# Two graph layers in fp32: the products of Q and K issued with 128 moving columns instead of 256

## The chip, the cores and the metric

The kernel runs on one core of a Trainium2 chip. The metric is the device time of one execution in microseconds (us). The engines are called as the profile calls them: PE is the matrix engine (its MATMUL instructions), PEld is its other row, on which the weight loads (LDWEIGHTS) stand, DVE is the vector engine, ACT the scalar engine, POOL is GpSimd, and SP is the engine whose queue issues most of the transfers.

## What is computed

There are 64 graphs of 256 nodes with 512 features, and an adjacency matrix of 256 x 256 for each. Two attention layers follow one another; all data are fp32.

```
# layer 0: one score per pair of nodes, masked by adj
feat_proj = feats @ fc_w.T + fc_b
logits = q(feat_proj) + k(feat_proj)^T ;  masked = leaky(logits + (1 - adj) * -1e9)
x1 = softmax(masked) @ feat_proj + feats
# layer 1: eight heads of 64
Q = x1 @ W_q + b_q ; K = x1 @ W_k + b_k ; V = x1 @ W_v + b_v
scores = Q_h @ K_h^T / 8 + (a_i + c_j + b_g) + log(adj + 1e-9)
out = softmax(scores) @ V_h (heads side by side) + x1
```

## The kernel before

**Tiling.** Two graphs make a group of 512 tokens, so there are 32 groups. Every pass of the main loop (`step`, L1107) works on up to four groups at once: it finishes group d, does layer 1 of group a, layer 0 of group f and loads group n. The order of all instructions on all engines is written out by hand: `attention_and_layer_0` (L1068) and `step` issue pieces such as `pq.p7` or `factor:2:0` one after the other, and each engine carries out its own instructions in that order.

**The big products.** Four products of 512 tokens x 512 features x 512 features are made for a group: pf (layer 0 features), pq (Q), pk (K) and pv (V). Each is done as a 2 x 2 block product with seven instead of eight block products (Strassen's scheme in Winograd's form). A block is 256 x 256. DVE makes the sums of blocks beforehand (`xsum`, L374, and `ysum`, L349) and adds the results afterwards (`sum`, L442). `Product.add` (L401) issues one block product: two halves m of 128 output rows, two steps k of 128 along the contraction, so 4 calls of `matmul` (L412), each with a stationary block of 128 x 128 and 256 moving columns. With `rows` true (pf and pv) the tokens are stationary and the weights move; with `rows` false (pq and pk) a block of weights is stationary and the 256 columns that move are tokens: 128 of each of the two tiles t of a graph (TPG is 2). The result of a block product fills one PSUM bank: two halves m of 256 columns each. Where the moving block is a block of x1 itself, its columns lie in pieces of 32 (`moving`, L380), else in rows of 128 (`by_chunks`, L361).

Each call of `matmul` on fp32 data becomes two pairs on the chip, each pair a LDWEIGHTS and a MATMUL: the profile counts 512 MATMULs for a kind of pq product of which the program issues 8 calls in each of 32 groups.

**What stands around pq and pk in the order.** In `step`, after pf has ended, comes `pq.p1 pq.keep_1 pk.p1 pk.keep_1 pv.p1 pv.keep_1`, then the remaining block products of pq and pk in the order p6, p7, p2, p5, p3, p4 of pq, mixed with those of pk (L1131 to L1148), then pv. After each, ACT copies the bank (`read`, L426) or DVE adds it to a copy (`sum`, L442). PSUM has a pool of four banks (`bank`, L179) and a pool of two pairs of banks (`pair`, L182). Layer 1 goes on with the scores (`sc`, L859), the exponential on ACT (L873), the multiplication with the adjacency on DVE (L879) and the product with V (`oT`, L899). Layer 0 makes `y` (L689) and then pf. A small product `rc` (L637), with 80 moving columns, makes sums of weights. In the first group there are transposes by PE (`xTp` L705, `pfc` L152, `qrow` L581, `x1Tp` L811), each with 128 moving columns[...].

Of the kernel before, what the change touches and what calls it, by code (L numbers as in the profile page):

```python
# [17 lines left out]
P = 128  # L18
# [7 lines left out]
def kernel(  # L26
# [64 lines left out]
    nc = tc.nc  # L91
# [3 lines left out]
    B = 32  # L95
    RS = P // 4
    NC = D // P
    TPG = N // P
# [65 lines left out]
    def fast():  # L164
        main = ExitStack()
        with main:
# [222 lines left out]
            class Product:  # L389
# [11 lines left out]
                def add(self, n, dst, start):  # L401

                    a, b = a_w[self.a][n], self.b[n]
                    l, r = (b, a) if self.rows else (a, b)
                    for m in range(2):
                        for k in range(2):
                            o, lk, rk = dst[:, m], l[:, k], r[:, k]
                            if len(rk.shape) == 3:
                                o = o.rearrange("p (t n) -> p t n", t=TPG)
                            elif len(rk.shape) == 4:  # L410
                                o = o.rearrange("p (t a m) -> p t a m", t=TPG, m=B)
                            nc.tensor.matmul(  # L412
                                o, lhsT=lk[:, ts(m, P)] if len(lk.shape) == 2 else lk[:, m], rhs=rk,
                                start=(start and m == 0 and k == 0), stop=(m == 1 and k == 1),
                                skip_group_check=True,
                            )

                def fresh(self, n, scores=False):
                    name = f"{self.name}_{n}"
# [750 lines left out]
            with tc.manual_schedule(engines=ENGINES):  # L1170
# [9 lines left out]
                d, a, a_w = None, None, {}  # L1180
                for g in range(NG):
                    n = Group(g + 1) if g + 1 < NG else None
# [7 lines left out]
                    d, a, f = a, f, n  # L1190
# [215 lines left out]
```

## Time and profile before

| what | value |
|---|---|
| time, median of 2 runs | 2311.41 us (2310.98 and 2311.84) |
| span of the profiled execution, first to last instruction | 2308.8 us |
| time of the profiled execution itself | one of the two runs; the page gives only its span, 2.2 to 3.0 us under their times |
| PE busy (MATMUL) | 2294.2 us, 99% of the span, 12618 instructions |
| PEld busy (LDWEIGHTS) | 1905.2 us, 83%, 12618 instructions |
| DVE busy | 2124.2 us, 92% |
| ACT busy | 1071.8 us, 46% |
| POOL busy | 121.9 us, 5% |
| mean share of the 16 DMA engines, queue q1 | 28.8% |
| mean granted clock of PE | 0.997 of full speed |

How to read the profile: a line of a group gives the line of the program, the engine, the operation, what it writes and reads, the number of instructions, and behind the bars the busy time in us with the mean of one in ns, and the idle time of the engine just before them. For PE the duration of a MATMUL goes from its start to a modelled end, and consecutive MATMULs overlap; so the time that a MATMUL costs in a stream is the distance from one start to the next, which the timeline and the chain of work give, and not the duration of one. In the timeline a row "start, us, engine, line, operation, xcount" covers count instructions from the first start to the last end; with the duration of one known, the distance of two starts is (us minus the duration of one) divided by (count minus 1).

### The profile page before, as it was taken

To read this page: it belongs to the slowest core of one execution; us is meant where nothing else is said; L and a number is where in the kernel's file an instruction comes from. 1 tells how busy PE (TensorE), PEld (TensorE's weight loads), DVE (VectorE), ACT (ScalarE), POOL (GpSimd) and SP (SyncE) were. 2 spreads that over 40 slices of the span, in tenths; PEclk is the share of its full clock that TensorE was granted. 3 is DMA by queue.
4 is the path that set the end of the run, shared out by engine and by line. 5 is a ranking of instruction groups with operands and counts; after the bars stand their busy time and mean duration, and the time that the engine had idled before them with its cause. 6 is when DMAs were issued, how large, how long until landed. Compare 5 with 4: busy or idle time off the path is not lost.

```text
span 2308.8 us, 33613 instructions
## 1 busy us (share of the span) xinstructions
PE 2294.2 (99%) x12618; PEld 1905.2 (83%) x12618; DVE 2124.2 (92%) x3180; ACT 1071.8 (46%) x1865; POOL 121.9 (5%) x120
## 2 busy tenths in 40 slices
PE   9999999999999999999999999999999999999997
PEld 6888888888888888888888888888888888888885
DVE  6899999999999999999999999999999999999997
ACT  3544444454445444454444454444544445444443
POOL 0000000000000000000000000000000000000000
PEclk9999999999999999999999999999999999999999
DMA  4122332223322233232233232332222323223312
GB/s 133 46 61 73 78 76 66 70 61 85 79 73 61 61 78 78 74 68 61 69 78 83 60 75 63 79 78 74 64 60 74 78 73 70 65 64 81 84 46 38
DMA packets 517264, 163.84 MB, mean 71 GB/s; under 512 B 415188, under 2 KB 478696, under 8 KB 517096
## 3 DMA queue, kind: packets, MB, share of 16 engines
q1 hardware_dynamic: 514440, 160.32, 28.8%
q8 instruction: 102, 1.67, 0.3%
q10 hardware_dynamic: 2656, 1.31, 0.2%
q14 instruction: 66, 0.54, 0.1%
HBM read 95.43 MB, written 66.12 MB: 70 GB/s over the span
## 4 chain that ended last, share of the span: by engine, by line
PE 98%; DVE 1%; DMA 0%; ACT 0%; issue 0%; ACTq 0%; DVEq 0%
PE pv L412 17%; PE pq L412 17%; PE pf L412 16%; PE pk L412 16%; PE sc L859 11%; PE oT L899 10%; PE y L689 9%; PE fp L718 1%; DMA fc_nat<-in_L_gnn_fc_w_dram 0%; PE rc L637 0%; DVE osb L1034 0%; PE tot L927 0%; DVE osb L1040 0%; PE xTp L705 0%; DVE osb L1033 0%; DVE x L756 0%
## 5 line engine op out<-in xcount | busy, mean ns | idle before, releaser
L873 ACT ACTIVATE e<-sc,c 128x1024 f32<-128x1024 f32 x254 | 269.0, 1110 | 79.2 <-PE sc L859 77.6
L879 DVE TENSOR_TENSOR e<-e,am 128x1024 f32<-128x1024 f32 x254 | 297.7, 1213 | 0.4 <-ACT e L873 0.4
L859 PE MATMUL sc<-qT,kT 64*128 64x256 f32 x2048 | 255.8, 390 | 0.3 <-ACT e L873 0.3
L899 PE MATMUL oT<-e,v 128*64 128x256 f32 x2032 | 233.4, 382 | 0.0
L859 PEld LDWEIGHTS sc<-qT,kT 64*128 64x128 f32 x2048 | 187.3, 187 | 52.6 <-issue 32.7
L495 POOL TENSOR_TENSOR pf_s<-pf_s,x 128x512 f32<-128x512 f32 x93 | 118.4, 1273 | 2106.1 <-ACT pf_s L494 2038.8
L689 PE MATMUL y<-e,x 128*128 128x256 f32 x992 | 225.6, 381 | 0.0
L899 PEld LDWEIGHTS oT<-e,v 128*64 128x64 f32 x2032 | 140.2, 137 | 85.3 <-issue 10.7
L689 PEld LDWEIGHTS y<-e,x 128*128 128x128 f32 x992 | 186.4, 190 | 23.7
L432 ACT ACTIVATE pq_s<-pq,cols 128x256 f32<-128x256 f32 x192 | 80.5, 470 | 249.1 <-PE pq L412 249.1
L494 ACT ACTIVATE pf_s<-pf,recip 128x256 f32<-128x256 f32 x186 | 77.9, 470 | 197.6 <-PE pf L412 197.6
L917 DVE TENSOR_REDUCE part<-est 128x32 f32<-128x1024 f32 x124 | 151.3, 1220 | 4.3
L916 DVE STREAM_TRANSPOSE est<-es 128x1024 f32<-128x1024 f32 x124 | 152.2, 1227 | 0.0
L886 DVE TENSOR_TENSOR es<-e,e 128x1024 f32<-128x1024 f32 x126 | 149.3, 1205 | 1.1
L695 ACT COPY yT<-y 128x512 f32<-128x512 f32 x124 | 72.6, 585 | 131.7 <-PE y L689 130.9
L429 ACT COPY pk_s<-pk 128x512 f32<-128x512 f32 x96 | 56.3, 586 | 165.7 <-PE pk L412 159.0
L906 ACT COPY oTs<-oT 128x512 f32<-128x512 f32 x128 | 75.0, 586 | 118.0 <-PE oT L899 97.3
L412 PE MATMUL pk<-t1b,wk 128*128 128x256 f32 x512 | 121.1, 380 | 0.4 <-DVE kT L443 0.4
L412 PE MATMUL pv<-wv,t1b_c 128*128 128x256 f32 x512 | 121.1, 380 | 0.0
L412 PE MATMUL pv<-wv,t1b 128*128 128x256 f32 x512 | 121.0, 380 | 0.0
L412 PE MATMUL pq<-x1T,wq 128*128 128x256 f32 x512 | 121.0, 379 | 0.0
L412 PE MATMUL pk<-x1T,wk 128*128 128x256 f32 x512 | 121.0, 379 | 0.0
(181 smaller groups left out, 4506.3 us busy)
## 6 DMA issues: line engine op xcount, KB each, us to landing
x<-in_x_dram SPq DMA_DIRECT2D x32, 1024.0 KB, 5.1
out_dram<-osb SPq DMA_DIRECT2D x254, 128.0 KB, 3.1
xd<-xt SPq DMA_DIRECT2D x124, 256.0 KB, 2.0
x1T<-xd SPq DMA_DIRECT2D x496, 64.0 KB, 1.9
adj<-in_adj_dram SPq DMA_DIRECT2D x128, 128.0 KB, 3.5
qrow<-q SPq DMA_DIRECT2D x31, 256.0 KB, 3.9
fc_nat<-in_L_gnn_fc_w_dram ACTq DMA_DIRECT2D x4, 256.0 KB, 3.8
wq<-in_L_gnn_W_q_dram SPq DMA_DIRECT2D x1, 1024.0 KB
```

The source lines that it names most:

```text
L412: nc.tensor.matmul(o, lhsT=lk[:, ts(m, P)] if len(lk.shape) == 2 else lk[:, m], rhs=rk, start=(start and m == 0 and k == 0), stop=(m == 1 ...
L432: nc.scalar.activation(dst[:, m], src[:, m], AF.Identity, bias=self.bias[:, 2 * o + m : 2 * o + m + 1],)
L494: nc.scalar.mul(s[:, m], src[:, m], self.recip[:, TPG * k + m : TPG * k + m + 1])
L495: nc.gpsimd.tensor_tensor(s, s, self.out(o, k), ALU.add)
L689: nc.tensor.matmul(y[:, ts(gr, N)], lhsT=self.x[:, gr * TPG + j, ts(c, P)], rhs=self.e0[:, j, gr, :], start=(gr == 0 and j == 0), stop=(gr ...
L859: nc.tensor.matmul(sc[:, par, pr, :], lhsT=self.kT[rows, 2 * hg + pr, ts(t, P)], rhs=self.qT[rows, 2 * hg + pr, ts(gr, N)], start=True, st ...
L873: nc.scalar.activation(e, sc, AF.Exp, bias=self.c[:, t : t + 1], scale=SCALE)
L879: nc.vector.tensor_tensor(ef, ef, self.am[:, jc, u // 2, :].unsqueeze(1).to_broadcast([P, 4, N]), ALU.mult,)
L886: nc.vector.tensor_tensor(self.esum[u], self.e[u, 0], self.e[u, 1], ALU.add)
L899: nc.tensor.matmul(oT[par * HD : (par + 1) * HD, pr, :], lhsT=self.v[:, gr * TPG + jc, ts(h, HD)], rhs=self.e[2 * gr + hg, jc][:, par, pr, :],
L916: nc.vector.transpose(turned, self.esum[u].rearrange("p a b i -> p (a b i)"))
L917: nc.vector.tensor_reduce(self.part[:, hg, :], turned.rearrange("p (m c) -> p m c", c=B), AX.X, ALU.add,)
```

## The change

In `Product.add`, for the products that are not `rows` (pq and pk), each call with 256 moving columns becomes two calls with 128 moving columns, one for each tile t of the graph. Both have the same stationary block, and each loads it for itself. They write the two halves of the columns that the one call wrote. The flag `start` stands on the first of them only where it stood before, and `stop` on the last. pf and pv are issued as before. No other engine's instructions and no order of pieces is changed.

```diff
                         for k in range(2):
                             o, lk, rk = dst[:, m], l[:, k], r[:, k]
-                            if len(rk.shape) == 3:
-                                o = o.rearrange("p (t n) -> p t n", t=TPG)
-                            elif len(rk.shape) == 4:
-                                o = o.rearrange("p (t a m) -> p t a m", t=TPG, m=B)
-                            nc.tensor.matmul(
-                                o, lhsT=lk[:, ts(m, P)] if len(lk.shape) == 2 else lk[:, m], rhs=rk,
-                                start=(start and m == 0 and k == 0), stop=(m == 1 and k == 1),
-                                skip_group_check=True,
-                            )
+                            lk = lk[:, ts(m, P)] if len(lk.shape) == 2 else lk[:, m]
+                            first, last = start and m == 0 and k == 0, m == 1 and k == 1
+                            if self.rows:
+                                nc.tensor.matmul(
+                                    o, lhsT=lk, rhs=rk, start=first, stop=last,
+                                    skip_group_check=True,
+                                )
+                                continue
+                            for t in range(TPG):
+                                ot = o[:, ts(t, P)]
+                                rt = rk[:, ts(t, P)] if len(rk.shape) == 2 else rk[:, t]
+                                if len(rt.shape) == 3:
+                                    ot = ot.rearrange("p (a m) -> p a m", m=B)
+                                nc.tensor.matmul(
+                                    ot, lhsT=lk, rhs=rt, start=first and t == 0,
+                                    stop=last and t == TPG - 1, skip_group_check=True,
+                                )
```

## The prediction

> **What bounds the kernel now.** I read the page's parts 1 and 4 first, then the chain of work in order of time for one middle group, then the rows of the weight loads, then the few places where PE already runs short matmuls.
>
> ```profile
> span 2308.8 us, 33613 instructions
> PE 2294.2 (99%) x12618; PEld 1905.2 (83%) x12618; DVE 2124.2 (92%) x3180; ACT 1071.8 (46%) x1865; POOL 121.9 (5%) x120
> PE 98%; DVE 1%; DMA 0%; ACT 0%; issue 0%; ACTq 0%; DVEq 0%
> ```
>
> The chain that ended last is PE for 98%. Busy time of PE says little by itself (ends are modelled), but the list of waits confirms it: PE's longest wait is 5.0 us, at the very end, and all its other waits together are under 5 us. DVE is busy for 92%, yet nobody waits for it long. So a microsecond more or less in PE's stream is a microsecond of the whole.
>
> ```profile
> 1037.97 6.91 PE pq L412 x32
> 1044.88 1.73 PE pk L412 x8
> 1046.60 3.45 PE pq L412 x16
> 1050.06 8.63 PE pk L412 x40
> ```
>
> These are pieces of the chain: start, length, count. Each is count x 216 ns (6.91 / 32 = 0.216), without gaps: the MATMULs of pq and pk follow each other every 216 ns. [...]
>
> ```profile
> L412 PEld LDWEIGHTS pq<-t1b,q_s 128*128 128x128 f32 x512 | 97.5, 190 | 13.0
> L412 PEld LDWEIGHTS pk<-x1T,k_s 128*128 128x128 f32 x256 | 48.7, 190 | 6.5
> ```
>
> Each MATMUL has its own load of 128 x 128, of 190 ns, which starts when the MATMUL before it starts and lies wholly beside it. pq has rows of 512 (x1T,wq), 512 (t1b,wq), 512 (t1b,q_s) and 256 (x1T,q_s): 1792. pk has the same. Together 3584 pairs, 3584 x 0.216 = 774.1 us, a third of the span.
>
> [...]
>
> **What the change does, part by part.** The listing of the changed program has, for pq and pk, eight 128 x 128 calls where there were four of 128 x 256, in the same places with the same waits; ACT, DVE, POOL and SP have their instructions in the old order, and no transfer is added but the fetching of a longer PE program. So:
>
> 1. Streaming: 3584 MATMULs of 216 become 7168 [...]. The transposes show it:
>
> ```profile
> 37.44 0.60 PE L811 MATMUL x1Tp<-ident,x 128*128 128x128 f32 x4
> ```
>
> Four starts in 0.60 us with 273 ns for the last: (0.60 - 0.273) / 3 = 109 ns. Streaming alone: 7168 x 109.2 = 782.7 us, 8.6 more than 774.1. The columns are the same[...].
>
> 2. Loads: 3584 more, and the cover for each halves from 216 to 109 ns. A transpose's load takes only 140 ns, so it is not proof for the 190 ns kind. Two places are nearer. Behind those transposes come ordinary loads:
>
> ```profile
> 37.44 0.36 PEld L811 LDWEIGHTS x1Tp<-ident,x 128*128 128x128 f32 x3 [0.29 <-issue]
> 37.77 0.30 PEld L750 LDWEIGHTS x1p<-v,e 128*128 128x128 f32 x2
> ```
>
> The two x1p loads take 0.30 us together, and each lasts about 190 ns, so they start 110 ns apart: the second starts as its predecessor's weights go into use, under a transpose of 128 columns. The other is the small product rc, with 80 columns (69 ns of streaming), where the load and not the stream must be the limit:
>
> ```profile
> 1008.90 0.41 PEld L637 LDWEIGHTS rc<-part,every 128*128 128x128 f32 x2
> 1009.23 0.30 PEld L689 LDWEIGHTS y<-e,x 128*128 128x128 f32 x2
> ```
>
> ```profile
> 1009.12 0.34 PE L637 MATMUL rc<-part,every 128*128 128x80 f32 x2
> 1009.30 0.42 PE L689 MATMUL y<-e,x 128*128 128x256 f32 x1
> ```
>
> The first rc load starts at 1008.90, the second 0.41 - 0.19 = 0.22 later (at 1009.12), y's first at 1009.23, its second 0.30 - 0.19 = 0.11 later. So with only 80 columns to hide in, full loads follow each other every 110 to 112 ns (all 31 groups show 109 to 113, read from the starts in ns); the y MATMUL lasts 0.42 instead of 0.38 us because it waits for its load, 0.04. [...] So a load occupies its path for about 111 ns[...]. [...]
>
> ```profile
> 1.86 2.25 PEld L1176 LDWEIGHTS warm<-ident 128*128 128x128 f32 x10
> ```
>
> Ten loads of 334 ns each, fp32 128 x 128, before MATMULs of 128 columns: (2.25 - 0.334) / 9 = 213 ns apart. The page's clock row shows full speed here, but a load of 334 ns instead of 190 doesn't[...].
>
> I take 111 ns per new pair. Sum: 7168 x 111 = 795.6, minus 774.1 = +21.5 us. Ends of this row: 110 gives +14.4, 112 gives +28.7. Only rc's short runs show the fp32 load as limit at full clock, hence the bounds for a long stream: 109.2 below (+8.6), and above, [...] the whole 190 (+588). [...]
>
> 3. Everything else, costed at nothing: ACT and DVE read the banks as before. Each bank is ready 16 x 111 - 8 x 216 ns = 0.05 us later, and the next piece of PE comes that much later too. In the stretch 1030.8 to 1058.6 DVE is busy for 24.1 of 27.8 us; it gets about 0.6 us more room in every group. If a bank's reader were late by more than its cover, PE would wait for it, but a slower PE lengthens the cover. The end after the last PE product (some 10 us of DVE and stores) stays.
>
> 4. Fetching the program: queue q8 brings 1.67 MB in 102 packets, about PE's 25236 instructions; 7168 more are 0.46 MB on queues that are 0.3% busy. PE will take an instruction every 55 ns through pq and pk; oT does so already (32 pairs in 3.60 us, 56 ns an instruction) without a wait.
>
> Against the profiled execution: 2308.8 + 21.5 = 2330.3 us of span. The median of the runs is 2.6 above the span: 2311.4 + 21.5 = 2332.9 us, 0.9% more. A measurement of this kernel tells about 2% from no change, so this falls within 2%.
>
> **The rivals.**
>
> A (the forecast), 0.70: load-limited at 110 to 112, 2325.8 to 2340.1 us.
>
> B, 0.12: the steady stream is limited by the columns alone, 109.2: 2320 us. [...] Against: rc's 111. If the builder or PE dropped the second load of the same block (the change then not doing what it says) the time would be this one too[...].
>
> C, slower by over 2%, 0.12: in a long stream the loads are not overlapped. Place: each LDWEIGHTS of pq and pk. Price: [...] the full 190 ns gives 2899 us. It decides from 114.5 ns per pair on (+46 us). For it: the load's duration of 190[...]. Against: rc's 31 groups and x1p's 110.
>
> D, slower as well, 0.04: the longer program arrives late. 7168 instructions in packets of 16 KB are 28 more packets; at 3.8 us each (the median landing of fc_nat, as an estimate) and with PE standing still each time, +106 us on top of A, 2439 us. Against: oT's rate without a wait, and queues that are nearly idle.
>
> What remains, 0.02, is for what I don't see; half of it I give to faster.
>
> **How the numbers follow.** The likeliest is A at 111: 2332.9. Its own range is 2325 to 2341. The range for 8 in 10 takes in B below and C's milder edge above up to its deciding point: 2317 to 2357, which holds A and B, 0.82. Faster by over 2%: 0.01. Within 2%: A, B and the rest, 0.83. Slower: C and D, 0.16.
>
> **What will show it.** PEld's count goes to 16202 and so does PE's. A chain piece of pq with 16 MATMULs should last 1.78 us (A), 1.75 (B)[...], where 8 last 1.73 now. MATMULs of pq and pk should last about 275 ns (273 plus a wait of a few). pf, pv, y, sc and oT keep their 216 spacing, and no wait of PE for ACT or DVE grows. I am wrong if loads at full clock with no slack at all need more than the 112 that short runs show, or if waits between the banks' readers and PE appear.

## The result and the profile after

| | before | after |
|---|---|---|
| median time, first measurement | 2311.41 us (2 runs) | 2339.84 us (2338.61 and 2341.06) |
| ratio | | 1.0122, 95% interval 1.0103 to 1.0141 |
| median time, second measurement | 2311.53 us (9 runs) | 2338.36 us (4 runs) |
| ratio | | 1.0114, 95% interval 1.0099 to 1.0130 |
| span of the profiled execution | 2308.8 us | 2339.3 us |

The kernel is slower by 1.1 to 1.2%. The head of the page after:

```profile
span 2339.3 us, 40781 instructions
...
PE 2323.5 (99%) x16202; PEld 2023.4 (86%) x16202; DVE 2126.0 (91%) x3180; ACT 1071.9 (46%) x1865; POOL 121.9 (5%) x120
...
q8 instruction: 129, 2.11, 0.4%
...
PE 98%; DVE 1%; DMA 1%; ACT 0%; issue 0%; SPq 0%; DVEq 0%
```

Both rows of PE have 3584 instructions more, the other engines none. The longer program is 27 packets more on q8 (the queue that brings the instructions), and the chain is still PE for 98%. The same pieces of the chain of one group, in order of time (start, length, engine, what, line, count):

```profile
1052.84 7.14 PE pq L421 x64
1059.98 1.79 PE pk L421 x16
1061.77 3.57 PE pq L421 x32
1065.34 8.93 PE pk L421 x80
1074.28 6.91 PE pv L411 x32
```

Now pq's 64 MATMULs take 7.14 us, 111.6 ns each, where 32 took 6.91; pv, which was not cut, keeps 216 ns (6.91 / 32). From the starts in the trace, in ns, 99% of the distances between MATMULs of pq and pk are 111 or 112; two of three are 112, so the mean is 111.67 ns. Before it was 215.83. The weight loads, by form:

```profile
L421 PEld LDWEIGHTS pq<-t1b,q_s 128*128 128x128 f32 x1024 | 119.4, 192 | 1.7
L421 PEld LDWEIGHTS pk<-t1b,k_s 128*128 128x128 f32 x1024 | 119.5, 192 | 0.0
```

The idle time before these loads, 13.0 us a row before, is all but gone (1.7 and 0.0), and as each load lasts 192 ns and they start 111.67 apart, consecutive ones overlap. For the MATMULs of pq the page after has 275 ns each, 3 more than the 272 to 273 of a transpose with as many columns. That fits a wait of 2.5 ns of each for its load (111.67 against 109.2, the mean distance of the transposes of both kernels at full clock).

The sum of the difference: from the first MATMUL of pq to the last of oT the profiled executions take 2253.4 us before and 2280.6 after, +27.2; 7168 x 111.67 - 3584 x 215.83 = 800.4 - 773.5 = +26.9. The first pq starts 3.1 us later in this execution (46.37 after 43.31). That belongs to this execution's start and not to the change: another profiled execution of the changed kernel, in the second measurement, started it at 43.83 and took 2280.6 us for the same stretch. About 1.4 us of the 3.1 are there when the first transposes of x start (10.99 after 9.55), with 1.2 us of waits for arriving data (0.3 before). Most of the rest comes up to 19.90 (16.85 before): between 16 and 20 us the granted clock was 0.52, and 1.00 before. The tail differs by 0.2 us.

### The profile page after: what moved, and what is told of

Read it like the earlier page. It is cut to its first block, busy times and chain, and to the rows that moved or that the text cites. A ratio compares the mean times of both kernels' runs of the same rounds, so it can differ in the third digit from the quotient of the medians.

```text
span 2339.3 us, 40781 instructions
## 1 busy us (share of the span) xinstructions
PE 2323.5 (99%) x16202; PEld 2023.4 (86%) x16202; DVE 2126.0 (91%) x3180; ACT 1071.9 (46%) x1865; POOL 121.9 (5%) x120
## 4 chain that ended last, share of the span: by engine, by line
PE 98%; DVE 1%; DMA 1%; ACT 0%; issue 0%; SPq 0%; DVEq 0%
PE pq L421 17%; PE pv L411 17%; PE pk L421 17%; PE pf L411 16%; PE sc L867 10%; PE oT L907 10%; PE y L697 9%; PE fp L726 1%; DMA x<-in_x_dram 0%; PE rc L645 0%; DMA xd<-xt 0%; PE pfc L152 0%; PE xTp L713 0%; DVE osb L1042 0%; PE tot L935 0%; DVE osb L1048 0%
## 5 line engine op out<-in xcount | busy, mean ns | idle before, releaser
L451 DVE TENSOR_TENSOR qT<-pq,pq_s 128x512 f32<-128x512 f32 x96 | 66.1, 689 | 64.9 <-PE pq L421 33.7
L421 PE MATMUL pq<-x1T,wq 128*128 128x128 f32 x1024 | 124.9, 275 | 0.2 <-DMA x1T<-xd 0.2
L421 PE MATMUL pk<-t1b,wk 128*128 128x128 f32 x1024 | 124.9, 275 | 0.2 <-DVE kT L451 0.2
L421 PE MATMUL pk<-x1T,wk 128*128 128x128 f32 x1024 | 124.8, 275 | 0.0
L421 PE MATMUL pq<-t1b,wq 128*128 128x128 f32 x1024 | 124.8, 275 | 0.0
```

The source lines that it names most:

```text
L421: nc.tensor.matmul(ot, lhsT=lk, rhs=rt, start=first and t == 0, stop=last and t == TPG - 1, skip_group_check=True,)
```

## The experiments

Theory 1: a pair of LDWEIGHTS and MATMUL costs the larger of two times, streaming (0.833 x N + 2.5 ns for N moving columns) and the load of the next block (0.833 x c + 5 ns for c stationary columns). The first is a line through the 215.83 ns of 256 columns and the 109.2 of the transposes with 128; two more distances of the kernel before lie on it, 69 ns between the two MATMULs of rc (80 columns, by the line 69.2) and 429 between those of fp (512 columns, 429.2). The second is an estimate: 111.67 at 128 columns is the change's, and its slope was taken to be that of the first, for no other width of a load had been measured as a limit. For 128 and 128 the two times are 109.2 and 111.7 ns, so the load decides. Theory 2: the load is hidden, and every MATMUL of the cut products has a fixed 5 ns above its columns (111.67 less 128 x 0.833). Theory 3: the supply of PE's instructions sets the pace.

The code below shows the lines that matter, without their indentation; `...` stands for lines left out.

**Uneven pieces.** As many pairs and columns as in the change, but 192 + 64, from both tiles t (where x1 itself moves, three and one of its four pieces of 32):

```diff
-for t in range(TPG):
-    ot = o[:, ts(t, P)]
-    rt = rk[:, ts(t, P)] if len(rk.shape) == 2 else rk[:, t]
...
+o = o.rearrange("p (t n) -> p t n", t=TPG)
+pieces = [(o[:, :, s], rk[:, :, s]) for s in (slice(0, 96), slice(96, 128))]
...
```

> Q's and K's calls of 256 columns are cut into 192 + 64 instead of 128 + 128; same number of pairs, loads and columns as in the change. Theory 1 [...]: [...] the 64 pairs are held at 111.7 ns by the load behind them; 3584 x (162.5 + 111.7) - 3584 x 215.8 = +209 us, about 2520 us. Theory 2 (each MATMUL costs its columns plus a fixed 5 ns, whatever the load): same as the change, +27 us, about 2339 us.

Measured: 2519.6 us, before 2311.5; ratio 1.0901, interval 1.0881 to 1.0921; +208.1 where theory 1 had +209 and theory 2 +27. The chain of this kernel:

```profile
1053.30 8.72 PE pq L427 x64
1062.02 2.19 PE pk L427 x16
```

136.3 ns for each MATMUL in the mean, the mean of 162.5 and 111.7 being 137.1 (the edges of a piece of the chain take off a little). By form, in the same kernel:

```profile
L427 PE MATMUL pq<-t1b,q_s 128*128 128x192 f32 x512 | 137.6, 350 | 0.0
L427 PE MATMUL pq<-t1b,q_s 128*128 128x64 f32 x512 | 84.7, 247 | 0.0
```

The starts in ns show how the halves of a call interleave. Each call makes two pairs with the same columns, so the order is 192, 192, 64, 64. The distance after a 192 is 162 or 163 when a 64 comes next, and 218 or 219 when a 192 does (63 times in 1792, at the head of a run, 162 or 163); it is 55 or 56 from a 64 to a 64, and 111 or 112 from a 64 to a 192. By theory 1 they should be 162.5, 162.5, 111.7 and 111.7; the start noted for a MATMUL behind a 64 comes early, as with rc (its second MATMUL starts 69 ns after the first, though the load of 190 ns in front of it began only with the first), so only the sum counts: 162.5 + 218.3 + 55.8 + 111.7 = 548.3, which is what theory 1 has. So the same number of pairs, loads and columns costs 180 us more once a part of the pairs has only 64 columns to cover a load. Theory 2 falls. (The 55.8 ns from a 64 to a 64 are the 0.833 x 64 + 2.5 of streaming.)

**Quarters.** Four pieces of 64 columns (32 from each tile t), against the uneven kernel:

```diff
-pieces = [(o[:, :, s], rk[:, :, s]) for s in (slice(0, 96), slice(96, 128))]
+pieces = [(o[:, :, s], rk[:, :, s]) for s in [ts(n, B) for n in range(4)]]
...
```

> The calls are cut into four of 64 columns, 14336 pairs instead of 3584, each with a full load. Theory 1 (load-limited, 111.7 ns per pair whatever the columns): 14336 x 111.67 - 773.5 = +827 us, about 3139 us. Theory 2 (columns plus fixed 5 ns): 14336 x 58.3 - 773.5 = +63 us, about 2374 us. Theory 3 (it is the supply of instructions to PE that sets the pace): at most as slow as theory 1, and the same time with shorter loads.

Measured: 3137.9 us; ratio 1.3577, interval 1.3552 to 1.3601; +826.4, theory 1 had +827. Half the columns per pair, the same time per pair (14.24 / 128 = 111.3 ns):

```profile
1012.32 3.57 PE pk L427 x32
...
1017.68 14.24 PE pq L427 x128
1031.91 3.57 PE pk L427 x32
```

**Shorter loads.** The change with 96 stationary columns in most calls:

```diff
+c = P if start and k == 0 else 96
...
-ot, lhsT=lk, rhs=rt, start=first and t == 0,
+ot[0:c], lhsT=lk[:, 0:c], rhs=rt, start=first and t == 0,
```

> As the change (128 + 128 columns), but each load and MATMUL of Q and K has only 96 stationary columns, except the 6 of 28 calls that begin a bank; a quarter of most sums of Q and K is left out. Theory 1: [...] these pairs go at 109.2 ns: 5632 x 109.17 + 1536 x 111.67 - 773.5 = +12.8 us, about 2324 us. Theory 2 (fixed cost per MATMUL) and theory 3 (instructions): as the change, +27 us, about 2339 us.

Measured: 2325.1 us, ratio 1.0060, interval 1.0047 to 1.0074; +13.6, theory 1 had +12.8 and the others +27. In the chain, pq's 32 at one go are now 3.49 / 32 = 109.1 ns each, the 109.2 of streaming; pk's first 16, half of which have full loads, lie between at 1.77 / 16 = 110.6:

```profile
1111.89 1.77 PE pk L426 x16
...
1115.39 7.03 PE pq L426 x64
1122.41 1.75 PE pk L426 x16
1124.16 3.49 PE pq L426 x32
```

From the starts in ns, a 96-wide pair is followed after 109 or 110 ns and a 128-wide one after 111 or 112. So two prices make up the change's 26.9 us: 3584 more MATMULs at 2.5 ns each, 9.0 us (7168 x 109.17 - 773.5), which stay when the loads are short, and 7168 x 2.5 ns = 17.9 us because full loads follow each other every 111.67 ns where 128 columns stream in 109.17. Of the 13.6 left here, 12.8 are the 9.0 and the 1536 pairs that kept their full loads (3.8); the interval is wider than the rest. In this kernel the MATMULs are narrower too, not only the loads. That the load is the cause fits the transposes of the kernel before: 128 wide, with 128 columns and shorter loads of 140 ns, they follow each other every 109 ns.

**Quarters with shorter loads.** Four pieces of 64 columns with 64 stationary columns, `c = P if start and k == 0 else 64`.

> Four calls of 64 columns as in the quarters kernel, with loads and MATMULs of only 64 stationary columns except the 6 of 28 calls that begin a bank; half of most sums of Q and K is left out. Theory 1: [...] 11264 x 58.3 + 3072 x 111.7 - 773.5 = +226 us, about 2538 us. Theory 2: as the quarters kernel by theory 2, about 2374 us. Theory 3 (supply of instructions): as the quarters kernel measures, since the instructions are as many.

Measured: 2657.1 us, ratio 1.1496, interval 1.1475 to 1.1517; +345.6, which none of the theories had. Theory 3 falls (345.6 against the quarters' 826.4 with as many instructions). Theory 1 is right in the steady stretches, where MATMULs 64 wide follow each other every 58 or 59 ns (theory 1 has 58.3 for the load and 55.8 for streaming), but short by 119 us in all. The surplus sits where the stationary width changes between 128 and 64: 205 ns from the last 128-wide to the first 64-wide MATMUL, 152 the other way, and once more 107 or 160 behind. There are 832 such changes, 143 ns each. The 96-wide loads showed nothing of the sort. This made a theory 4: a change between 128 and 64 stationary columns can't be covered.

**Widths that change with every call, and seldom.** Both kernels are the kernel before, with 256 moving columns, but for the width of Q's and K's calls:

```diff
+c = P if self.rows or k == 0 else P // 2               # alternating
+c = P if self.rows or (start and k == 0) else P // 2   # mostly 64
...
-o, lhsT=lk[:, ts(m, P)] if len(lk.shape) == 2 else lk[:, m], rhs=rk,
...
+o[0:c], lhsT=lk[:, 0:c], rhs=rk, start=first, stop=last,
```

> The kernel before with its 256 moving columns, but in Q's and K's products every call with k = 1 has only 64 of the 128 stationary columns (half of those sums is left out), so the width changes with every call: 4 changes in each of 448 block products, 1792 in all; 1792 of 3584 pairs have the shorter load. Theory 4 (a change of the stationary width between 128 and 64 can't be covered: the load behind it waits for the running MATMUL; 143 ns per change from the surplus of the quarters-with-64 kernel, 119 us over 832 changes, and 100 to 200 ns as the scores' pieces of the kernel before show): +180 to +360 us. Rival (the 64-wide loads themselves were slow in that kernel): here they hide under 216 ns of streaming, so 0 us.

> As the alternating kernel, with 256 moving columns, but 64 stationary columns in all of Q's and K's calls except the 6 of 28 that begin a bank: 2816 of 3584 pairs have the shorter load (half of these sums is left out), with only 832 changes of width. Theory 4: 832 / 1792 of what the alternating kernel loses, +83 to +166 us. Rival (short loads are slow): 2816 / 1792 = 1.6 times what it loses.

Measured: 2616.6 us, ratio 1.1322 (1.1289 to 1.1355), and 2451.6 us, ratio 1.0608 (1.0577 to 1.0639). That is +305.4 and +140.5 over the 2311.1 of before. The ratio of the two is 2.17, that of the numbers of changes 2.15; per change 170 and 169 ns. The rival had 0, or more in the second. How a change looks in the timeline of the weight loads of the alternating kernel:

```profile
1019.94 0.19 PEld L415 LDWEIGHTS pq<-x1T,wq 128*64 128x64 f32 x2 [0.33 <-issue]
1020.52 0.30 PEld L415 LDWEIGHTS pq<-t1b,wq 128*128 128x128 f32 x2 [0.39 <-issue]
1021.14 0.19 PEld L415 LDWEIGHTS pq<-t1b,wq 128*64 128x64 f32 x2 [0.33 <-issue]
```

In front of every change the row of the loads is idle for 0.33 to 0.39 us, although no engine is waited for ("issue"): in the kernel before, a load starts 1 or 2 ns after the MATMUL in front of it, but here a load of another width starts 308 ns after. From the starts in ns, that MATMUL is followed after 309 instead of 216, and the first one of the new width after 320 (128 wide) or 266 to 267 (64 wide): 93 ns, and then 104 or 51.

**One product alone, the other two, and all four.**

```diff
-if self.rows:
+if self.rows or self.name.startswith("pk"):   # Q only
+if not self.rows:                             # the products of layer 0 and V only
...
```

For all four, the branch that leaves a call whole is taken out.

> Only Q's products are cut in two, K's are as before. Theory 1 (each new pair costs 111.67 ns and nothing else changes): half of the change, 3584 x 111.67 - 1792 x 215.83 = +13.4 us, about 2325 us. Rival (part of the change's 28 us is a wait or a later start that either product brings): not half, but near 0 or near the whole 28 us.

> The products of layer 0 and V are cut in two (the weights that move, 256 to 128 columns, the tokens are loaded twice), Q and K are as before. Theory 1: 3528 calls' pairs become 7056: 7056 x 111.67 - 3528 x 215.83 = +26.5 us, about 2338 us, although other data stand and move and other engines work beside it. Rival (the price depends on the neighbours of Q and K or on the tokens' layout): another number, by more than 5 us.

> All four products are cut in two. Theory 1: the sum of both, 26.9 + 26.5 = +53.4 us, about 2365 us. Rival (DVE, busy for over nine tenths, or the readers of the banks give back or add time once PE is slower everywhere): clearly less or more than the sum.

> The change itself beside the others on the same chip. Theory 1: 7168 x 111.67 - 3584 x 215.83 = +26.9 us on the stretch of the groups; a difference of start times of some us can come on top, so 2336 to 2341 us, ratio 1.0116.

Measured against 2311.5 us: Q alone 2326.4 (1.0064; 1.0050 to 1.0078), +14.8 for +13.4 expected; layer 0 and V 2340.2 (1.0120; 1.0105 to 1.0136), +28.7 for +26.5; all four 2365.1 (1.0229; 1.0214 to 1.0245), +53.5 for +53.4; the change again 2338.4, +26.8 for +26.9. The price is the same per pair in products that keep their weights standing and in those that keep the tokens standing, and it adds up. DVE, at nine tenths busy, gave nothing back. It added a little, most in the kernel with layer 0 and V cut:

```profile
PE pk L415 <- DVE kT L455: 3.2, 4, 1.4
```

Four times in its profiled execution PE stood still before a block product of pk, until DVE had made the sum kT, 3.2 us in all (the two longest at 281 and 354 us); before, it did so once, for 0.4. This execution is the slowest of the four (2342.3 us), and the waits are most of what it has above the 26.5 us. The others were not profiled, so that the 2 us of surplus in the median are the same wait is likely, not shown; 26.5 lies inside the interval. With all four products cut there is one such wait of 0.2 us.

## Why the prediction was right

Its likeliest case came, near that case's upper edge (+28.4 and +26.8 us measured, +21.5 predicted, its own range +14.4 to +28.7). The size was 5 us short, and the +28.4 fits into the range only just.

**What bounds the kernel** (a microsecond in PE's stream is one of the whole): right. +26.9 us of stream are +27.2 in the stretch and +26.8 in the second measurement, and all four products added up.

**Streaming, step 1** (109.2 ns, at least 8.6 us): right; shown by the kernel with 96-wide loads, 109.1 to 109.4 ns in its chain.

**Loads, step 2** (full loads follow each other every 110 to 112 ns, though each lasts 190): right, and that the load decides is shown by the uneven pieces (+208.1 us), the quarters (+826.4) and the 96-wide loads (+13.6). The size was a little off: I took 111 as the mean of what rc's short runs show, and a long stream runs at 111.67. With 7168 pairs, the 0.67 is 4.8 us; the rest of the difference to 26.9 is that I charged 216 ns for the pairs before, 0.17 too much, 0.6 us. rc had shown it: of its two tight distances, the first (110) begins with a load that came 216 ns after the one before it, and only the second (111 or 112) has a tight load on both sides. The second was the one to take. The loads of the six matmuls at the very start (`warm`), 213 ns apart, are no witness for this. In the changed kernel transposes, whose loads don't decide at full clock (109.2 ns), are 213 apart too where the granted clock was 0.50 (14 to 16 us), and for that clock twice the 111.67, an estimate, would be 223.

**Everything else at nothing, steps 3 and 4:** right for this change. PE's longest wait is still the 5.0 us at the end, and its other waits are under 2 us each. The quarters with 64-wide loads took a pair every 58.3 ns, so an instruction every 29, where the prediction asked for one every 55. That a reader of a bank can come late, as step 3 had it, was seen with layer 0 and V cut: 3.2 us of 2342.

**The rivals.** B (streaming limits, 2320 us) fell by 2.5 ns per pair. C (loads not overlapped) fell: loads of 192 ns start 111.67 ns apart, and a pair costs 2.5 ns more than its columns alone. D (the program arrives late) fell with the quarters: four times as many pairs, 84 packets more on q8 than before, and +826.4 us where the loads alone make +827.

## What to carry to other kernels

Before cutting a matmul, or merging two, compare the time that the moving columns stream with the closest distance of two loads, not with the load's duration in the profile: here loads of 192 ns followed each other every 111.7 ns, and with as many columns moving as standing the load decided by a little (111.7 ns against 109.2 for 128 and 128, and 58.3 against 55.8 for 64 and 64). In this stream, which bounds the kernel, the cut cost 2.5 ns per added MATMUL even where the load was hidden (the 96-wide loads), and with 64 moving columns and full loads each added pair cost 111.7 ns. To find that distance in a kernel whose loads are all hidden, look for the one short matmul (here rc, with 80 columns), and read the distance that has a tight load on both sides (111 or 112 ns).

## What the runs showed of the hardware

Distances in a steady fp32 stream at full clock: 215.8 ns for 256 moving columns, 109.2 for 128 with short loads, and where the load decides, 111.7 ns for 128 stationary columns and 58.3 for 64.

Not expected: changing between 128 and 64 stationary columns costs 170 ns on the mean of both directions in the kernel with 256 moving columns, although a MATMUL's 216 ns are longer than either load (188 ns of 128 columns, 134 of 64). A load behind a change of width between 128 and 64 starts 308 ns after the start of the last MATMUL; one behind a change between 128 and 96 isn't held back (109 to 112 ns from MATMUL to MATMUL). The kernel before pays the like at its own changes of shape. Its score products (sc) stand on 64 rows, oT has 64 stationary columns:

```profile
1025.25 3.60 PE oT L899 x32
1028.85 0.09 PE tot L927 x4
1028.94 1.93 PE sc L859 x16
1030.87 1.93 PE pf L412 x8
1032.79 1.73 PE pq L412 x8
```

From the chain of the kernel before: 16 MATMULs of sc, two of which start within 7 ns of each other, would take 8 x 216 = 1728 ns and take 1930. The 128 such pieces are 26 us. The pieces behind them pay again: pf's 8 MATMULs take 1.93 us where pq's 8, with no change in front, take 1.73, and oT's 32, also two within 7 ns, take 3.60 where 16 x 216 ns is 3.46. With 66 pieces of the first kind (pv and pf) and 61 of the second that is an estimated 22 us more, so some 48 us or 2% of the span in all, more than the change of this document. That it is the same cause as with the widths is a reading of the like distances, not tried: 309 ns from the last MATMUL of pv, pf or oT to sc and then 320 from pair to pair; 306 from sc to pf and then 320; 306 from sc to oT and then 267. An order with fewer changes of shape was not tried either.
